# Gathering the last rows of eight experts by quarter, and starting a quarter's attention when its own tiles are added

## The chip, the cores and the metric

The kernel runs on one core of a Trainium2 chip. The core has five engines that run their own instruction streams: TensorE (PE, matmuls, with its weight loads listed as PEld), VectorE (DVE), ScalarE (ACT), GpSimd (POOL) and SyncE (SP, which here only issues DMA transfers). The metric is the device time of one execution in microseconds (us); lower is better.

## The reference

A residual stream `x` of 4 sequences of 1024 rows of 128 numbers passes four layers. Each layer is `x = norm(x + mixer(x))`, then `x = norm(x + ffn(x))`. The change lies at the seam between the last two layers, so only these matter:

```python
# layer 2, FFN: 8 experts, top 2 of each row
x = _layernorm(x + _L2_ffn_ref(x, ...))
# layer 3, attention: a gated unit whose mixing over time is a Toeplitz product
x = _layernorm(x + _L3_attn_ref(x, ...))
# layer 3, FFN: 32 experts, top 4 of each row, and a shared gated unit
logits = flat @ router_w.T + router_bias
scores = softmax(logits)
topk_scores, topk_idx = top_k(scores, 4)
topk_scores = topk_scores / topk_scores.sum(-1)
h = silu(einsum('nd,ehd->neh', flat, gate_w)) * einsum('nd,ehd->neh', flat, up_w)
expert_out = einsum('neh,edh->ned', h, down_w)
out = sum of the 4 chosen expert_out, times topk_scores
out = out + silu(flat @ sgate_w.T) * (flat @ sup_w.T) @ sdown_w.T
x = _layernorm(x + out)
```

The layer-3 attention takes the first axis, the four sequences, as the axis that it mixes over: a row meets only the rows of the same step in the other sequences. So a quarter of the 1024 steps (256 steps of all four sequences) can pass through it by itself, as soon as all four sequences have those steps. The layer-2 attention before it works along each sequence.

## The kernel before

`x` stays in SBUF as 32 tiles of 128 rows. Eight tiles make a quarter: two of each of the four sequences. All weights are loaded by SP when they are needed.

**Experts.** For an FFN with experts, a part of the rows goes through fixed steps. The router writes, for each row and each of its k choices, a position in a list (`pos...`, written on DVE at L1272) and a weight (`wk...`). `spread` scatters the rows of `x` to the list in DRAM, one POOL transfer of 128 rows for each tile and choice. The experts read the list four tiles at a time (`xg`), one group after the other, and write results to a second list (`yg`). `collect` gathers the results back, again one POOL transfer (L1297) for each tile and choice into a buffer `yt`, and adds them to `x` on DVE with their weights (L1388).

**Parts.** Layer 2 splits the rows three ways: `a2` is the first two quarters of all sequences, `m2` the last two quarters of sequences 0 and 1, `n2` the last two quarters of sequences 2 and 3. With two choices, `n2` has eight tiles and 16 gathers. Its tiles 0 and 1 are the third quarter of sequence 2, tiles 2 and 3 the fourth quarter of sequence 2, tiles 4 and 5 the third quarter of sequence 3, and tiles 6 and 7 the fourth quarter of sequence 3. Layer 3 splits by time: part `a` is quarters one and two, `b` the third quarter, `c` the fourth. A part of layer 3 passes, in this order, `l3_attn` (norm, root mean square, projections, mixing over the sequences, projection, second norm, transposes), `l3_route` (logits, softmax, the mask of the top four, positions), `spread` (64 scatters for `a`, 32 each for `b` and `c`), `l3_shared` (the shared unit, with its products `hs`), `l3_experts` (20 groups for `a`, 12 each for `b` and `c`, then a branch at L1355 for rows that overflow), `collect` and the final norm.

**Order.** Each step is a Python generator that emits some instructions and yields an estimated cost in us. `mix(main, side, pace)` emits the main step and, each time main has spent its cost, as much of the side work. `chain` runs generators one after the other; `abreast` runs several and always continues the one whose sum of costs is smallest. `collect` keeps the gathered tiles in a queue and adds a tile when its gathers are thought to have landed or when the pool's buffers are used up. The engines execute in the emitted order, each its own stream, and wait for each other by semaphores.

The seam looks like this. While `mix` emits the shared unit and the experts of part `a`, the side work is the chain of L1918 to L1927: the collection of `n2`, the attention and the routing of `b`, and what follows.

```python
on = self.chain(
    on, self.rows_in(n2), self.l3_attn(b), self.l3_route(b),
    self.abreast(
        self.chain(self.spread("l3", b, K3), self.when(listed("made l3a")), self.last(a, yp)),
        self.chain(self.l3_attn(c), self.l3_route(c)),
    ),
```

`rows_in(part)` opens a pool of its own with eight buffers on the right side of SBUF and calls `collect`. Such pools are closed again when the part is done, so the next one takes the same memory: the buffers for `n2` lie where those for `m2` lay. `yp` is the pool `l3y`, with eight buffers on the left side, opened just before this chain and used for the collections of layer 3.

The names in the profile: `yt<-l2yn` is a gather of `n2`'s results, `x<-yt,wkl2n` its add; `bn<-x` (L191) is the first instruction of a norm; `lg` are the router's logits (L1658 the sum with the bias, L712 the end of the softmax); `posl3b` are the positions of part b; `l3rb<-x` a scatter of part b's rows; `xg<-l3rb` the load of a group of its list; `gu`, `hg`, `hT` and `yp` are an expert group's products in the order of the work (gate and up, gated, transposed, down).

Of the kernel before, what the change touches and what calls it, by code (L numbers as in the profile page):

```python
# [41 lines left out]
E2, F2, R2, K2 = 8, 512, 16, 2  # L42
# [32 lines left out]
class Kernel:  # L75
# [1298 lines left out]
                        in_=self.zero.unsqueeze(1).to_broadcast([P, tl - at, D]),  # L1374
                    )

    def collect(self, lay, part, k, yp, first=0, nt=None):

        nc = self.nc
        pos, wk = self.route[lay + part.name][:2]  # L1380
        assert f"made {lay}{part.name}" in self.listed
        ys = self.lists[lay, part.name][1]
        late = []

        def add():
            t, yt, _ = late.pop(0)
            for i in range(k):
                nc.vector.scalar_tensor_tensor(  # L1388
                    self.x[:, part.order[t], :], yt[:, i, :], wk[:, t, i : i + 1], self.x[:, part.order[t], :],
                    ALU.mult, ALU.add,  # L1390
                )

        for t in range(first, first + (nt or part.nt)):
            yt = self.tile(yp, [P, k, D], "yt")
            for i in range(k):
                self.indirect(
                    out=yt[:, i, :], out_offset=None, in_=ys,
                    in_offset=bass.IndirectOffsetOnAxis(ap=pos[:, t, i : i + 1], axis=0),
                )

            late.append((t, yt, self.moved_by + 4.0))
            if len(late) == yp.bufs:
                while late[0][2] > self.now:
                    yield (1.0,)
                add()
            yield (1.26 * k,)
        while late:
            while late[0][2] > self.now:
                yield (1.0,)
            add()  # L1410
            yield (0.36 * k,)
# [456 lines left out]
    def all(self):  # L1868
        a, rest = self.first, self.rest
        b, c = rest  # L1870
        r = self.both[1]
        a2, m2, n2 = self.by_rows
        with ExitStack() as ctx:
            lgp = self.pool(ctx, "l2lg")
            self.l2_lg = self.tile(lgp, [P, NT, E2], "lg")
            with ExitStack() as early:

                self.l0_setup(early)
                self.l2_wr = self.load(lgp, self.ins["l2_wr"])
                self.run(self.l0_attn((0, 1)))  # L1880
                self.l1_setup()
                self.l2_setup()
                self.zero_lists("l1")
                self.run(self.l0_ffn((0, 1)))
                self.run(self.l1_attn((0, 1)))

                self.run(self.l1_route(a))
                self.run(self.mix(self.l0_attn((2, 3), True), self.spread("l1", a, K1)))
                self.zero_lists("l2", "l3")
                with ExitStack() as c2:  # L1890
                    wall = self.l1_wall(c2)
                    yp = self.pool(c2, "l1ya", 5, right=True)
                    side = self.chain(self.l0_ffn((2, 3), True), self.l1_attn((2, 3), True))
                    self.run(self.mix(self.chain(self.l1_shared(a), self.l1_experts(a, wall)), side, 2.0, False))
                    self.run(self.mix(self.abreast(self.l2_weights(), side), self.l1_close(a, yp)))
            with ExitStack() as c2:
                wall = self.l1_wall(c2)
                self.run(self.mix(self.l2_attn(0), self.chain(self.l1_route(r), self.spread("l1", r, K1))))
                wall2 = self.l2_wall(c2)
                yp = self.pool(c2, "l1yr", 5, right=True)  # L1900
                self.run(self.mix(self.chain(self.l1_experts(r, wall), self.l1_shared(r)), self.routed(a2)))
                self.run(self.mix(self.l2_experts(a2, wall2), self.l1_close(r, yp)))
            listed = lambda name: lambda: name in self.listed
            on = self.served(
                self.chain(self.rows_in(a2), self.onward(a, True)),
                (lambda: self.rows_done >= B + 2, self.routed(m2)),
                (lambda: self.rows_done == 2 * B, self.routed(n2)),
            )
            self.run(self.mix(self.l2_attn(1), on, drain=False))
            with ExitStack() as c3:  # L1910
                with ExitStack() as c2:
                    wall = self.l2_wall(c2)
                    self.press(on, listed("l2m"))
                    self.run(self.mix(self.l2_experts(m2, wall), on, drain=False))
                    self.press(on, lambda: {"l2n", "routed l3a"} <= self.listed)
                    sw, wall3 = self.l3_wall(c3, True)
                    on = self.chain(on, self.rows_in(m2))
                    self.run(self.mix(self.l2_experts(n2, wall), on, drain=False))  # L1918
                self.press(on, listed("l3a"))
                yp = self.pool(c3, "l3y", 8)  # L1920
                on = self.chain(
                    on, self.rows_in(n2), self.l3_attn(b), self.l3_route(b),
                    self.abreast(
                        self.chain(self.spread("l3", b, K3), self.when(listed("made l3a")), self.last(a, yp)),
                        self.chain(self.l3_attn(c), self.l3_route(c)),
                    ),
                    self.spread("l3", c, K3), self.when(listed("made l3b")), self.last(b, yp),  # L1927
                )
                self.run(self.mix(self.chain(self.l3_shared(a, sw), self.l3_experts(a, wall3)), on, 0.75, False))
                self.press(on, listed("l3b"))  # L1930
                self.run(self.mix(self.chain(self.l3_shared(b, sw), self.l3_experts(b, wall3)), on, 0.75, False))
                self.press(on, listed("l3c"))
                self.run(self.mix(self.chain(self.l3_shared(c, sw), self.l3_experts(c, wall3)), on))
                self.run(self.close(c, yp))
        bad = self.nc.values_load(self.flag[0:1, 0:1], min_val=0, max_val=1)
        with self.tc.If(bad > 0):
            with ExitStack() as ctx:
                lgp = self.pool(ctx, "l2lg2")
                self.l2_lg = self.tile(lgp, [P, NT, E2], "lg")
                self.l2_wr = self.load(lgp, self.ins["l2_wr"])  # L1940
                self.l2_attn_general()
                for p in self.by_rows:
                    self.run(self.routed(p))
                    with ExitStack() as c2:
                        self.run(self.l2_experts(p, self.l2_wall(c2)))
                    self.run(self.rows_in(p))
                for p in self.parts:
                    self.run(self.onward(p))
                    with ExitStack() as c2:
                        sw, wall = self.l3_wall(c2)  # L1950
                        self.run(self.l3_shared(p, sw), self.l3_experts(p, wall))
                        self.run(self.last(p, self.pool(c2, "l3y" + p.name, 5)))
# [165 lines left out]
```

## Time and profile before

| | us |
|---|---|
| median of three runs | 2064.29 |
| lowest, highest | 2057.93, 2067.41 |
| profiled execution, its own time | 2440.36 |
| its span, first to last instruction | 2438.2 |
| PE busy in the span | 1619.9 |
| DVE busy | 1303.3 |
| ACT busy | 789.9 |
| POOL busy | 774.0 |

The profile is one execution with the recorder on. It took 376 us, or 18%, more than the median, so its times place the work and size the steps, and only their sum can be held against its own 2440.36 us. A line of a list of groups gives the source line, the engine, the operation, output and inputs with their names, and how many; in a timeline the first two numbers are start and length in us, and a number in brackets is idle time of that engine just before, with what ended it.

The last stages in that execution: shared unit of part a until 1935.3 us; experts of part a 1941.5 to 2034.1; routing of part b until 2063.7; scatters of part b 2064.1 to 2105.1; experts of part b 2109.6 to 2231; gathers of part a 2105.4 to 2228.3; scatters of part c 2228.6 to 2273.1; gathers of part b 2273.4 to 2313.2; experts of part c until 2379.6; gathers of part c 2384.3 to 2424.

### The profile page before, as it was taken

Reading aid. Unit: us, or ns where it says so; the run is one execution under the profiler, and the core shown is the slowest. Engines: PE = TensorE matmul, PEld = TensorE weight load, DVE = VectorE, ACT = ScalarE, POOL = GpSimd, SP = SyncE. Lnnn points to the kernel's source line nnn. Section 1 sums busy time; section 2 is a strip of 40 time slices with the busy share of each in tenths; the row PEclk is TensorE's granted clock in tenths of the full one; section 3 lists DMA queues with packets and bytes.
Section 4 is the critical chain, followed back from the end, with each engine's and each line's share of the span. In section 5 each row is a group of like instructions: output and inputs, shape, how many; then the busy total and the mean of one; then the engine's idle time right before and its main releaser. Section 6 shows DMA issues by size and latency. Waiting matters only on the chain. (4 is left out here: it accounts for less than half of the span.)

```text
span 2438.2 us, 27135 instructions
## 1 busy us (share of the span) xinstructions
PE 1619.9 (66%) x9017; PEld 962.6 (39%) x9017; DVE 1303.3 (53%) x3732; ACT 789.9 (32%) x1114; POOL 774.0 (32%) x701
## 2 busy tenths in 40 slices
PE   7535776875661775687968787887853898267080
PEld 3214333753320344545623232345532586154070
DVE  8767795655570564324535665464711378247053
ACT  5511372322230432222336454642211254122030
POOL 5531285145227002224132002002164201736704
PEclk9766787988785888888979898988876998577595
DMA  9930002334101014312120000031141141223132
GB/s 308 288 104 0 13 33 82 117 120 159 60 31 52 14 73 142 100 48 70 44 96 21 1 1 17 2 117 35 42 174 40 44 127 45 71 71 96 51 100 59
DMA packets 215530, 187.10 MB, mean 77 GB/s; under 512 B 16528, under 2 KB 194064, under 8 KB 214864
## 3 DMA queue, kind: packets, MB, share of 16 engines
q1 hardware_dynamic: 194672, 142.29, 18.5%
q0 software_dynamic: 20704, 42.86, 5.7%
q8 instruction: 84, 1.38, 0.2%
q14 instruction: 70, 0.57, 0.1%
HBM read 88.49 MB, written 96.60 MB: 76 GB/s over the span
## 5 line engine op out<-in xcount | busy, mean ns | idle before, releaser
L1051 ACT ACTIVATE pr<-sc 128x1024 f32<-128x1024 f32 x288 | 279.6, 1021 | 326.1 <-PE sc L157 197.7
L157 PE MATMUL gu<-ld,xgT 128*128 x640 | 172.1, 413 | 81.9 <-issue 36.6
L157 PE MATMUL sc<-qm,kT 32*128 32x512 f32 (+3 forms) x1536 | 200.2, 564 | 15.9 <-ACT pr L1051 12.0
L157 PE MATMUL s<-pr,va 128*32 128x512 f32 (+3 forms) x1536 | 177.3, 531 | 46.0 <-issue 27.9
L157 PEld LDWEIGHTS gu<-ld,xgT 128*128 128x128 f32 x640 | 123.6, 204 | 109.5 <-issue 48.0
L157 PE MATMUL gu<-wall,xgT 128*128 x304 | 161.0, 657 | 3.2 <-ACT xgT L167 2.0
L1057 DVE TENSOR_TENSOR pr<-pr,ld 128x512 f32<-128x512 f32 (+1 forms) x160 | 92.5, 581 | 101.3 <-ACT pr L1051 98.8
L169 DVE COPY hT<-tp 128x512 f32<-128x512 f32 x118 | 81.0, 686 | 120.7 <-PE tp L165 50.4
L165 PE MATMUL tp<-ld,hg 128*128 128x128 f32 x624 | 100.6, 285 | 50.4 <-DVE hT L169 35.4
L157 PEld LDWEIGHTS sc<-qm,kT 32*128 32x128 f32 x1536 | 85.5, 200 | 119.5 <-issue 66.6
L165 PE MATMUL tp<-ld,xg 128*128 128x128 f32 x396 | 66.3, 295 | 90.9 <-issue 50.7
L165 PEld LDWEIGHTS tp<-ld,hg 128*128 128x128 f32 x624 | 80.1, 147 | 104.8 <-DVE hT L169 42.2
L167 ACT COPY xgT<-tp 128x512 f32<-128x512 f32 x99 | 58.0, 587 | 195.4 <-PE tp L165 126.9
L1730 DVE TENSOR_TENSOR hg<-sg,gu 128x256 f32<-128x256 f32 x160 | 65.7, 416 | 102.5 <-ACT sg L1729 94.8
L1494 ACT ACTIVATE sg<-gu 128x512 f32<-128x512 f32 x76 | 45.2, 597 | 226.3 <-PE gu L157 115.3
L1297 POOL DMA_INDIRECT l1ra<-x,posl1a x64 | 95.6, 1494 | 60.5 <-DVE posl1a L1272 41.3
L1729 ACT ACTIVATE sg<-gu 128x256 f32<-128x256 f32 x160 | 60.6, 384 | 157.3 <-PE gu L157 85.7
L157 PE MATMUL pu<-xT,ld 128*128 128x512 f32 x104 | 65.0, 719 | 60.1 <-issue 58.5
L1297 POOL DMA_INDIRECT yt<-l1yr,posl1r x64 | 60.7, 948 | 139.2 <-DVE x L1388 78.8
L157 PEld LDWEIGHTS s<-pr,va 128*32 128x32 f32 x1536 | 38.7, 113 | 156.6 <-issue 110.6
L1496 DVE TENSOR_TENSOR hg<-sg,gu 128x512 f32<-128x512 f32 x76 | 51.8, 681 | 87.2 <-ACT sg L1494 43.9
L1297 POOL DMA_INDIRECT l1rr<-x,posl1r x64 | 61.7, 964 | 99.6 <-DVE posl1r L1272 80.4
(443 smaller groups left out, 3551.7 us busy)
## 6 DMA issues: line engine op xcount, KB each, us to landing
wall<-wall SPq DMA_DIRECT2D x16, 768.0 KB
l3ra<-zero SPq DMA_DIRECT2D x1, 6144.0 KB
ld<-in_l_w SPq DMA_DIRECT2D x2, 3072.0 KB
wall<-we SPq DMA_DIRECT2D x24, 256.0 KB
ld<-in_l_w SPq DMA_DIRECT2D x1, 6144.0 KB
l1ra<-zero SPq DMA_DIRECT2D x1, 5120.0 KB
l1rr<-zero SPq DMA_DIRECT2D x1, 5120.0 KB
xg<-l3ra SPq DMA_DIRECT2D x20, 256.0 KB
```

Of the source, the lines that this page charges most:

```text
L157: return self.nc.tensor.matmul(out, lhsT, rhs, start=start, stop=stop)
L165: nc.tensor.transpose(pt[:, k * P : (k + 1) * P], s, self.ident)
L167: nc.scalar.copy(dst, pt[:, : n * P])
L169: nc.vector.tensor_copy(dst, pt[:, : n * P])
L1051: nc.scalar.activation(pr, sc[h], AF.Exp)
L1057: nc.vector.tensor_tensor(d, d, cst["tril"].unsqueeze(1).unsqueeze(1).to_broadcast([P, 2, n, P]), ALU.mult)
L1297: ins = self.nc.gpsimd.indirect_dma_start(**kw)
L1494: nc.scalar.activation(sg, gu[:, 0, :], AF.Silu)
L1496: nc.vector.tensor_tensor(h, sg, gu[:, 1, :], ALU.mult)
L1729: nc.scalar.activation(sg, pg[:, :, 0, :], AF.Silu)
L1730: nc.vector.tensor_tensor(h[:, 2 * c : 2 * c + 2, :], sg, pg[:, :, 1, :], ALU.mult)
```

## The change

`collect` takes a list of tiles. The chain of L1918 no longer calls `rows_in(n2)`. It collects the four tiles of the third quarter first; then the attention and the routing of part b run abreast with the collection of the four tiles of the fourth quarter. Both collections use the pool `yp` instead of a pool of their own.

```diff
-    def collect(self, lay, part, k, yp, first=0, nt=None):
+    def collect(self, lay, part, k, yp, first=0, nt=None, which=None):
...
-        for t in range(first, first + (nt or part.nt)):
+        for t in which or range(first, first + (nt or part.nt)):
             yt = self.tile(yp, [P, k, D], "yt")
...
                 yp = self.pool(c3, "l3y", 8)
+
                 on = self.chain(
-                    on, self.rows_in(n2), self.l3_attn(b), self.l3_route(b),
+                    on, self.collect("l2", n2, K2, yp, which=(0, 1, 4, 5)),
+                    self.abreast(
+                        self.chain(self.l3_attn(b), self.l3_route(b)),
+                        self.collect("l2", n2, K2, yp, which=(2, 3, 6, 7)),
+                    ),
                     self.abreast(
                         self.chain(self.spread("l3", b, K3), self.when(listed("made l3a")), self.last(a, yp)),
                         self.chain(self.l3_attn(c), self.l3_route(c)),
```

## The prediction

> **What bounds the kernel now.** I read the page's totals first, then the windows of the last 650 us, then one tile's waits, then timelines around the two edges of the change.
>
> ```profile
> PE 1619.9 (66%) x9017; PEld 962.6 (39%) x9017; DVE 1303.3 (53%) x3732; ACT 789.9 (32%) x1114; POOL 774.0 (32%) x701
> q8 instruction: 84, 1.38, 0.2%
> ```
>
> No engine is busy throughout, so the bound must be read stage by stage. The rows below give a stretch, its length, and the busy us of PE, weight loads, DVE, ACT and POOL.
>
> ```profile
> 1800.00:1864.00 64.00, 6.97 (x31) 4.54 (x29) 2.66 (x4) 1.99 (x4) 48.11 (x51) 0.59 0.15 52
> 1893.00:1916.00 23.00, 23.00 (x102) 14.15 (x103) 7.31 (x12) 5.38 (x9) 0.00 (x0) 1.00 0.04 12
> 1916.00:1938.00 22.00, 19.13 (x92) 12.29 (x90) 8.64 (x20) 4.18 (x7) 11.47 (x12) 1.00 0.14 37
> 1941.00:2034.00 93.00, 87.16 (x536) 75.06 (x536) 64.12 (x169) 46.71 (x88) 3.06 (x4) 0.96 0.37 112
> 2036.00:2064.00 28.00, 24.64 (x89) 15.53 (x90) 22.08 (x110) 12.56 (x18) 0.00 (x0) 0.76 0.03 7
> 2064.00:2106.00 42.00, 15.51 (x58) 8.37 (x56) 12.57 (x27) 7.75 (x12) 32.15 (x33) 0.71 0.16 60
> ```
>
> Part a's 20 expert groups (1941 to 2034) are PE's: 87 us busy of 93. Then from 2036 to 2064 the path is part b's attention tail and routing on DVE, and from 2064 to 2106 POOL's scatters of part b's rows. What releases POOL there decides:
>
> ```profile
> L1297 POOL DMA_INDIRECT l3rb<-x,posl3b x32: 957/962/1262, 2064.1 to 2104.2; - x32
>   DVE posl3b L1272: 119.1, 1
> ```
>
> POOL stood idle 119.1 us for the positions of part b. After the scatters the expert inputs are loaded at 2106.5 and the rest (experts b, gathers a, scatters c, experts c, gathers c) follows in a chain. So the time moves with posl3b, at 2063.67. The timelines (start, length) show what sets it:
>
> ```profile
> 1969.95 0.34 DVE L1388 SCALAR_TENSOR_TENSOR x<-yt,wkl2n,x 128x128 f32<-128x128 f32 x1
> 1970.21 0.29 DVE L191 BATCH_NORM_STATS2 bn<-x 128x6 f32<-128x128 f32 x1
> ...
> 2046.56 0.42 DVE L1658 TENSOR_TENSOR lg<-s,rows 128x256 f32<-128x256 f32 x1 [0.88 <-PE s L157]
> 2049.77 0.42 DVE L712 TENSOR_TENSOR lg<-lg,red 128x256 f32<-128x256 f32 x1
> 2063.67 0.16 DVE L1272 TENSOR_SCALAR posl3b<-pm 128x32 uint32<-128x32 f32 x1
> ```
> ```profile
> 2033.05 1.06 PE L157 MATMUL yp<-ld,hT 128*128 x8
> 2039.36 2.18 PE L165 MATMUL s<-ld,x 128*128 128x128 f32 x8 [5.25 <-DVE x L205]
> ```
>
> The attention's first norm starts at 1970.2, behind the last of n2's 32 adds. Paced beside the experts, it is not done when PE finishes them (2034.1): its second norm still runs, PE waits 5.25 us for it, and transposes, logits and softmax follow with little cover.
>
> **What the Trainium skill says.** "Perfetto Trace Analysis", DMA Instruction — SWDGE (GPSIMD): the recorded end of such a POOL transfer is the end of descriptor generation, not the data's arrival. The trace agrees: the first gather of the last collection is recorded from 2384.25 for 0.95 us, and its add starts at 2386.83. So buffers free up later than POOL's rows tell. "ScalarE: Activation LUTs", What ACT_TABLE_LOAD costs: about 1.28 us a load plus a 1.38 us drain. The loads here are 1.28 us (1973.49, 1975.10); no separate drain shows (1973.49 + 1.28 = 1974.77, next activation at 1974.78), so I use 1.28. "Runtime: NRT & Kernel Launch", Instruction fetch mechanics: instructions stream in 16 KiB blocks over a DMA queue of the sequencer's own, mostly hidden. Block size agrees (1.38 MB / 84 = 16.4 KB). "Mostly hidden" does not hold beside POOL bursts: PE idles 54.0 us under "issue" at 2258.9, until part b's gathers end. That the burst delays the fetch is my inference.
>
> **The change, part by part.** The instruction list is the same on every engine within five; what changes is order, buffers and waits.
>
> Gathers: the 16 gathers of n2 (2 per tile, 1.25 us apart) stay in place on POOL, third-quarter tiles first. Their eight buffers now come from the left-side pool of the later gathers, not from the memory in which m2's rows lay. Before, they waited for DVE's adds of m2's rows:
>
> ```profile
> 1916.63 0.95 POOL L1297 DMA_INDIRECT yt<-l2yn,posl2n  x1 [53.29 <-DVE x L1388]
> 1927.07 1.07 POOL L1297 DMA_INDIRECT yt<-l2yn,posl2n  x1 [5.75 <-DVE x L1388]
> ```
>
> Afterwards the first needs only the list's last write (issued 1892.6, so about 1895), and all 16 can go in one run of 16 × 1.25 = 20 us, 1895 to 1915. Nothing on POOL is behind them until part b's scatters. Direct worth: zero, since DVE takes the rows up from 1955.8. Bounds: a gain of about 3, as the hold of the first expert input (last shared matmul about 1935.3, load issued 1938.53) ends just after today's burst; a loss is rival 2.
>
> Attention start: before, 16 adds of the fourth and third quarters lie in five batches behind groups' hT copies from 1955.8 to 1970.4. Afterwards the eight third-quarter adds go behind the first groups' copies and the norm starts behind the fourth group's, which in today's clock is about 1958.6: 11.6 us, 3.3 groups of 3.54 us. Its weights' loads (l3_uv, l3_o; 1970.59 and 1971.07) move on SP ahead of later expert-input loads, and there wait only for m2's gathers, done at 1863: cost zero, two issues of 0.38 us on a queue with a 3.5 us period. If that queue were late, the fourth input load slips by under 1 us.
>
> The other eight adds: 8 × 0.27 = 2.2 us, now between the attention's rms steps, where DVE is nearly full (1970 to 1992: 17.9 busy of 21.8). The lead at the attention's end is 11.6 − 2.2 = about 9.5 us, before the branch that ends the experts (L1355).
>
> PE: eight transposes (about 0.9 us beside the expert stream) and eight logits matmuls (0.8) come ahead of the last `yp`: experts end at 2034.1 + 1.7. Table loads: the second norm's sqrt pair moves inside group 18; two loads, 2 × 1.28, half covered by the rotation of two buffers: +1.3. So about 2037.1. Then, in a row: lg add .42, reduce .41, subtract .42 behind it, load for exp 1.28, exp .42, reduce .41, reciprocal .20 = 3.6: L712 at 2040.7 against 2049.77, 9.1 earlier.
>
> L712 to posl3b took 13.9 us; five `hs` products of 0.69 lay in it and about 1.7 us of waits for PE. Those waits shrink, one product falls out, or neither: 11.6 to 13.9. posl3b at 2052.3 to 2054.6, an advance of 9.1 to 11.4; I take 10. If DVE's 5 us of second norm stays ahead of the branch's wait, 5; if the hold at 1935 goes too, about 14.
>
> Downstream it carries one to one: 32 scatters at 1.266 = 40.5 us need nothing else (POOL had been idle), part b's shared matmuls (26 us of PE) lie under them, then inputs, gathers (64 × 1.25 = 80), scatters c, experts c. What is late next is POOL.
>
> **Sum.** 2440.4 (span 2438.2) − 10 = 2430.4. The profiled execution is 376 us, 18%, above the median of 2064.3; which stages swell isn't shown. The stretch concerned has almost no POOL work and few idle gaps, so I carry the 10 us over whole; scaled by 2064/2440 it would be 8.5. Taken: 2054.
>
> **Rivals.**
> 1. The lead is eaten in the expert stage. For: DVE has 64 us busy of 93, 82% where the attention is dense, and each group waits for ACT's and DVE's turns. If the moved table loads, eight x-norms (2.1 us) and 2.2 us of adds stretch the groups in full, 10 − 1.3 − 2.1 − 2.2 = about 4 are left: 2060. Against: PE's idle in the stage is only 6 us, so most of DVE's work does fit.
> 2. Slower: the unbroken gather run of 1895 to 1915 falls on part a's shared matmuls, where PE is now 23.0 busy of 23, and starves PE or DVE of instructions. From 1824 to 1865 PE was busy 1.04 us of 41 beside 32 gathers. If PE stops for the run, up to 20 us are lost and the 10 gained don't pay: 2074. Decides when PE's busy share there falls below half. Against: beside today's 12 gathers (1916 to 1938) PE kept 19.1 of 22.
> 3. More: the hold at 1935 goes (3), PE's clock (0.76 after the branch) stays up because PE has no 5.25 us gap, and part c, ahead by the same order, also leaves its holds: 14 to 20 us, 2047.
> 4. It does nothing: posl3b doesn't move since routing is bound by the shared matmuls' `hs` on DVE; 2064. Against: they take 5 × 0.69 of 13.9.
>
> **How the numbers follow.** Forecast case 0.45 (2049 to 2059), rival 1 0.17, rival 2 0.16, rival 3 0.16, rival 4 0.06. A measurement of this kernel tells about 0.5%, 10.3 us, from no change. The forecast lies on that edge: three fifths of its chance counts as faster, two fifths as same. Faster: 0.27 + 0.16 and 0.02 of rival 1 = 0.45. Same: 0.18 + 0.15 + 0.06 less 0.02 of rival 4's tail = 0.37. Slower: 0.16 + 0.02 = 0.18. The range, 2041 to 2072, leaves out the upper part of rival 2 and the end of rival 3.
>
> **What would show it.** Right: gathers of l2yn in one run from about 1895; first BATCH_NORM_STATS2 after them near 1958; L1658 ahead of the branch; PE's 5.25 us wait gone; posl3b some 10 us before 2063.7, and every later stage by as much. Wrong: PE's idle between 1893 and 1938 above 3 us (rival 2), groups in 1941 to 2034 longer than 93 us in all by over 5 (rival 1), or posl3b early and the end not, which would put the bound on something I did not see behind it.

## The result, and the profile after

The changed kernel takes 2051.16 us (median of ten runs, 2045.74 to 2057.39), the kernel before 2060.54 (2051.75 to 2067.41). The ratio is 0.9958, interval 0.9940 to 0.9977: about 8.7 us faster, somewhere between 4.7 and 12.4.

The profile that the prediction was read from shows an execution of 2440 us, in a condition that these timed runs do not share, so below the changed kernel (its profiled execution took 2053.12 us, span 2051.1) is compared with a second profile of the kernel before, of 2055.36 us (span 2053.2). Both lie within the range of the timed runs, so the recorder is not what costs 18%.

The two spans differ by only 2.1 us, less than the 8.7 of the timed runs: part a's positions were written at 1530.6 us in the one and at 1535.0 in the other, ahead of everything that the change touches. Times are therefore counted from the load of part a's first expert input (1646.2 before, 1650.8 after). From there to the end of the span it is 407.0 us before and 400.3 after, 6.7 us less, which lies within the interval of the timed gain.

First the page's totals, before (second profile) and then after, and for the latter one of its two instruction queues (packets, MB, share).

```profile
PE 1542.9 (75%) x9017; PEld 930.7 (45%) x9017; DVE 1302.4 (63%) x3732; ACT 789.6 (38%) x1114; POOL 778.8 (38%) x701
```
```profile
PE 1542.7 (75%) x9017; PEld 927.7 (45%) x9017; DVE 1303.3 (64%) x3732; ACT 787.6 (38%) x1113; POOL 777.9 (38%) x701
q8 instruction: 84, 1.38, 0.3%
```

The engines do the same work; it only lies elsewhere. Next the stretches of the last gathers and shared unit, the experts of part a, the routing of part b, its scatters: before, then after (stretch, length, busy us of PE, weight loads, DVE, ACT, POOL, each with its count, then PE's granted clock as a share of full speed, the busy share of the DMA engines and GB/s).

```profile
1617.00:1646.20 29.20, 19.36 (x86) 12.33 (x86) 9.27 (x22) 3.58 (x6) 22.19 (x24) 0.76 0.20 55
1646.20:1742.70 96.50, 86.99 (x536) 74.70 (x536) 66.93 (x179) 47.65 (x90) 9.68 (x11) 0.96 0.40 118
1742.70:1771.00 28.30, 24.03 (x88) 15.27 (x89) 22.67 (x116) 13.23 (x18) 0.00 (x0) 0.76 0.05 13
1771.00:1813.00 42.00, 15.28 (x58) 8.47 (x56) 12.77 (x28) 7.96 (x12) 31.91 (x33) 0.70 0.16 59
```
```profile
1621.60:1650.80 29.20, 19.82 (x86) 12.52 (x86) 9.24 (x21) 3.58 (x6) 22.02 (x24) 0.75 0.18 53
1650.80:1751.70 100.90, 90.32 (x560) 77.36 (x560) 74.99 (x222) 52.72 (x97) 9.43 (x10) 0.97 0.38 114
1751.70:1768.00 16.30, 14.14 (x48) 8.00 (x49) 13.88 (x71) 5.52 (x8) 0.00 (x0) 0.79 0.06 18
1768.00:1810.00 42.00, 20.25 (x75) 11.22 (x74) 13.91 (x29) 8.69 (x13) 32.11 (x33) 0.76 0.17 60
```

Some 4 us more pass in the expert stage and 12 fewer in the routing. PE's records beside the experts rise from 536 to 560: eight transposes, and eight logits matmuls with two records each. DVE takes on 8.1 us in the stage (66.93 to 74.99), which grows by 4.4.

The edges of the change on DVE and PE, before (two views) and after (two views):

```profile
1677.81 0.29 DVE L191 BATCH_NORM_STATS2 bn<-x 128x6 f32<-128x128 f32 x1
...
1754.16 0.42 DVE L1658 TENSOR_TENSOR lg<-s,rows 128x256 f32<-128x256 f32 x1 [0.88 <-PE s L157]
1757.37 0.42 DVE L712 TENSOR_TENSOR lg<-lg,red 128x256 f32<-128x256 f32 x1
1770.89 0.16 DVE L1272 TENSOR_SCALAR posl3b<-pm 128x32 uint32<-128x32 f32 x1
```
```profile
1746.97 2.18 PE L165 MATMUL s<-ld,x 128*128 128x128 f32 x8 [5.27 <-DVE x L205]
```
```profile
1670.65 0.28 DVE L191 BATCH_NORM_STATS2 bn<-x 128x6 f32<-128x128 f32 x1
...
1749.68 0.42 DVE L1658 TENSOR_TENSOR lg<-s,rows 128x256 f32<-128x256 f32 x1 [1.01 <-PE s L157]
1753.80 0.43 DVE L712 TENSOR_TENSOR lg<-lg,red 128x256 f32<-128x256 f32 x1
1767.68 0.18 DVE L1272 TENSOR_SCALAR posl3b<-pm 128x32 uint32<-128x32 f32 x1
```
```profile
1745.57 1.04 PE L165 MATMUL s<-ld,x 128*128 128x128 f32 x8
1746.44 0.60 PE L165 MATMUL tp<-ld,hg 128*128 128x128 f32 x4
1746.88 1.06 PE L157 MATMUL yp<-ld,hT 128*128 x8
1747.77 1.87 PE L157 MATMUL s<-ld,xT 128*128 128x32 f32 x16
1749.47 1.14 PE L157 MATMUL yp<-ld,hT 128*128 x8
1753.86 2.05 PE L157 MATMUL pg<-xT,ld 128*128 128x512 f32 x2 [3.25 <-DVEq L1355]
```

Subtract the first input's load and the rows line up: the norm starts at 31.6 before and 19.9 after, L1658 at 108.0 and 98.9, L712 at 111.2 and 103.0, posl3b at 124.7 and 116.9. PE's 5.27 us wait for the attention is gone; in its place it waits 3.25 us at the branch for DVE (DVEq is DVE's instruction sequencer, L1355 the branch).

The first gather of n2, before and then after:

```profile
1639.27 0.95 POOL L1297 DMA_INDIRECT yt<-l2yn,posl2n  x1 [0.30 <-DVE x L1388]
```
```profile
1643.41 0.97 POOL L1297 DMA_INDIRECT yt<-l2yn,posl2n  x1 [0.30 <-PE pu L157]
```

It follows the last gather of m2 after 0.30 us in both, and the other fifteen follow it about 1.25 us apart. In neither kernel does POOL wait for DVE's adds of m2's rows here: the 53.29 us that the prediction showed belongs to the other condition. The scatters of part b answer for what follows.

```profile
L1297 POOL DMA_INDIRECT l3rb<-x,posl3b x32: 954/958/1260, 1771.3 to 1811.3; - x32
  DVE posl3b L1272: 112.4, 1
```
```profile
L1297 POOL DMA_INDIRECT l3rb<-x,posl3b x32: 954/958/1436, 1768.1 to 1807.9; - x32
  DVE posl3b L1272: 105.0, 1
```

They start at 125.2 before and 117.3 after, from the first expert input. From posl3b to the end of the span it is 282.3 us before and 283.4 after.

### The profile page after: what moved, and what is told of

The parts are those of the page before. It is cut to its first block, busy times and chain, and to the rows that moved or that the text cites. A ratio compares the mean times of both kernels' runs of the same rounds, so it can differ in the third digit from the quotient of the medians.

```text
span 2051.1 us, 27115 instructions
## 1 busy us (share of the span) xinstructions
PE 1542.7 (75%) x9017; PEld 927.7 (45%) x9017; DVE 1303.3 (64%) x3732; ACT 787.6 (38%) x1113; POOL 777.9 (38%) x701
## 2 busy tenths in 40 slices
DMA packets 215530, 187.10 MB, mean 91 GB/s; under 512 B 16528, under 2 KB 194064, under 8 KB 214864
## 5 line engine op out<-in xcount | busy, mean ns | idle before, releaser
L157 PE MATMUL sc<-qm,kT 32*128 32x512 f32 (+3 forms) x1536 | 190.0, 551 | 1.0 <-ACT pr L1051 1.0
L157 PE MATMUL gu<-ld,xgT 128*128 x640 | 167.2, 404 | 24.1 <-DVE hg L1730 12.5
L157 PE MATMUL s<-pr,va 128*32 128x512 f32 (+3 forms) x1536 | 164.7, 524 | 17.7 <-DVE x L989 7.3
L157 PE MATMUL gu<-wall,xgT 128*128 x304 | 147.8, 610 | 3.2 <-ACT xgT L167 2.0
L165 PE MATMUL tp<-ld,hg 128*128 128x128 f32 x624 | 96.3, 276 | 2.8 <-DVE hT L169 2.7
L1297 POOL DMA_INDIRECT l2rm<-x,posl2m x16 | 15.7, 984 | 200.4 <-DVE posl2m L1272 195.8
L1297 POOL DMA_INDIRECT l3ra<-x,posl3a x64 | 61.5, 962 | 77.1 <-DVE posl3a L1272 51.0
L157 PE MATMUL yp<-ld,hT 128*128 x640 | 86.0, 277 | 2.4 <-DVE hT L169 1.5
## 6 DMA issues: line engine op xcount, KB each, us to landing
wall<-wall SPq DMA_DIRECT2D x16, 768.0 KB, 10.6
ld<-in_l_w SPq DMA_DIRECT2D x2, 3072.0 KB, 13.5
```

The lines of the kernel that those rows point to most:

```text
L157: return self.nc.tensor.matmul(out, lhsT, rhs, start=start, stop=stop)
L165: nc.tensor.transpose(pt[:, k * P : (k + 1) * P], s, self.ident)
L1297: ins = self.nc.gpsimd.indirect_dma_start(**kw)
```

## The experiments

All ratios are to the kernel before in the same comparison. "posl3b at" is counted from the load of part a's first expert input.

**The kernel before once more.** No edit.

> The kernel before once more, for a profile that stands nearer to the timed runs than the one shown. Theory (the attention's lead sets posl3b): posl3b is written 8 to 11 us later, counted from the first expert input of part a, than in the changed kernel (113.4 us), so at 121 to 125; from posl3b to the end of the span as in the changed kernel, 283 us within 3. Rival (the freed gathers bring the gain): posl3b at 113 to 116 after the first expert input, and the shared unit of part a ends its first-input hold some 5 to 9 us later.

posl3b at 124.7, changed kernel 116.9: 7.8 us later, just under the 8 to 11 expected. The 113.4 us in the expectation was counted from PE's first transposes, 3.5 us after the load; the comparison is unaffected. From posl3b to the end it is 282.3, as expected. The theory holds; that the freed gathers bring the gain does not.

**Buffers and order apart.** Three kernels take the change's two halves apart.

```diff
 # only the buffers
-    on, self.rows_in(n2), self.l3_attn(b), self.l3_route(b),
+    on, self.collect("l2", n2, K2, yp), self.l3_attn(b), self.l3_route(b),
```

> Only the buffers change: n2's rows are collected in the old order and wholly ahead of the attention, but into the pool of layer 3, so the 16 gathers need not wait for DVE's adds of m2's rows. Theory (the attention's lead is the gain): ratio to before 0.999 to 1.001, at most 3 us faster by the hold ahead of the first expert input. Rival A (the freed gathers are the gain): 0.995 to 0.997. Rival B (the unbroken run of gathers starves the shared unit): 1.003 or more.

Ratio 1.0003 (0.9991 to 1.0016), posl3b at 125.1. The buffers are worth nothing here, where the kernel before does not wait for them.

```diff
 # only the order: a right-side pool as in rows_in
+    def split_in(self, part, b):
+        with ExitStack() as ctx:
+            yp = self.pool(ctx, "l2y" + part.name, 8, right=True)
+            yield from self.collect("l2", part, K2, yp, which=(0, 1, 4, 5))
+            yield from self.abreast(
+                self.chain(self.l3_attn(b), self.l3_route(b)),
+                self.collect("l2", part, K2, yp, which=(2, 3, 6, 7)),
+            )
...
-    on, self.collect("l2", n2, K2, yp, which=(0, 1, 4, 5)),
-    self.abreast(
-        self.chain(self.l3_attn(b), self.l3_route(b)),
-        self.collect("l2", n2, K2, yp, which=(2, 3, 6, 7)),
-    ),
+    on, self.split_in(n2, b),
```

> Only the order changes: third quarter first, attention begun when its own tiles are added, but the gathers keep a right-side pool of their own where m2's buffers lay and wait for DVE's adds as before. Theory (lead): ratio 0.995 to 0.997, the whole gain or all but 1 to 3 us of it. Rival A (freed gathers): 0.999 to 1.001, since the late gathers hold the adds and so the attention.

Ratio 0.9952 (0.9935 to 0.9970), posl3b at 116.1. The order brings the whole gain.

> The changed kernel once more, on the chip of the two partial kernels. Both theories: ratio 0.994 to 0.998, as measured first (0.9958). If the lead and the buffers add up, its gain is the sum of the gains of the two partial kernels within 2 us.

Ratio 0.9957 (0.9937 to 0.9978), posl3b at 117.0. In us of 2060.43: the buffers lose 0.6, the order gains 9.9, both together gain 8.9. They add up within the expected 2 us, though each of these figures is uncertain by 3 to 4 us; posl3b (125.1, 116.1, 117.0) tells the same more sharply.

```diff
 # third quarter first, but the attention behind all eight tiles
-    on, self.collect("l2", n2, K2, yp, which=(0, 1, 4, 5)),
-    self.abreast(
-        self.chain(self.l3_attn(b), self.l3_route(b)),
-        self.collect("l2", n2, K2, yp, which=(2, 3, 6, 7)),
-    ),
+    on, self.collect("l2", n2, K2, yp, which=(0, 1, 4, 5, 2, 3, 6, 7)),
+    self.l3_attn(b), self.l3_route(b),
```

> The changed kernel with the tiles in the new order and the pool of layer 3, but the attention of part b held back until all eight tiles of n2 are added. Theory (what counts is that the attention starts behind four tiles): the gain is gone, ratio to before 0.999 to 1.002, posl3b 124 to 126 us after the load of part a's first expert input (before 124.7, changed kernel 116.9). Rival (having the third quarter first is enough): ratio near 0.996, posl3b at 117 to 119.

Ratio 1.0013 (0.9997 to 1.0029), posl3b at 124.8. Gathering the third quarter first does nothing by itself; beginning the attention behind its four tiles brings the gain.

**The price of the eight later adds.** They are held back by a condition on the emission.

```diff
-            while late[0][2] > self.now:
+            while late[0][2] > self.now or not (until is None or until()):
...
-    self.collect("l2", n2, K2, yp, which=(2, 3, 6, 7)),
+    self.collect("l2", n2, K2, yp, which=(2, 3, 6, 7), until=lambda: self.now >= 1454.0),
```

> The changed kernel with the eight adds of the fourth quarter moved from the attention's root-mean-square steps to its mixing steps some seven groups later. If the adds cost the attention their own 2.2 us, as the prediction has it: posl3b 114.5 to 115.5 us after the first expert input and a ratio near 0.9947. If DVE's gaps hide them: 116.5 to 117.5 and 0.9957, as in the changed kernel.

posl3b at 117.0, ratio 0.9954 (0.9938 to 0.9970). Moved by some seven groups they change nothing at the end. Nor do they at the place that they leave: from the start of the norm to the end of the rms steps it takes 19.0 us in the changed kernel, 18.8 with the adds moved away, and 19.0 in the kernel before, where all but one are done when the norm begins.

**More lead.** Two ways to begin or finish the attention still earlier. `land` is the time that `collect` allows a gather before its add.

```diff
-    on, self.collect("l2", n2, K2, yp, which=(0, 1, 4, 5)),
+    on, self.collect("l2", n2, K2, yp, which=(0, 1, 4, 5), land=-5.0),   # was 4.0
```

> The changed kernel with the first four tiles' adds placed earlier (their assumed landing 9 us sooner), so that the attention starts two groups earlier. Theory (the lead carries over one to one): 2 x 3.5 = 7 us more, posl3b 109 to 112 us after the first expert input, ratio 0.992 to 0.993. Rival A (the expert stage has no room for more, the lead is eaten): posl3b 115 to 118, ratio 0.995 to 0.997. Rival B (the adds now wait for their gathers and hold the groups' DVE work): expert stage of part a longer by 3 us or more, ratio 0.997 or more.

```diff
-    self.run(self.mix(self.chain(self.l3_shared(a, sw), self.l3_experts(a, wall3)), on, 0.75, False))
+    self.run(self.mix(self.chain(self.l3_shared(a, sw), self.l3_experts(a, wall3)), on, 0.6, False))
```

> The changed kernel with the pace of the work beside part a's shared unit and experts changed from 0.75 to 0.6, so that more of the attention is placed beside each group. Theory (lead): the routing is placed 63 x 0.2 = 12.6 us of main work earlier, of which the denser groups give back 3 to 6: posl3b 106 to 112, ratio 0.990 to 0.994. Rival (DVE has no room): the last store of part a's experts goes from 100.5 to 106 or later, posl3b 114 or later, ratio 0.995 or more.

The earlier start: the norm begins at 13.6 instead of 19.9, 6.3 us sooner, and posl3b comes at 115.3, only 1.6 sooner. Ratio 0.9954 (0.9934 to 0.9974). The last store of the experts moves from 100.5 to 104.3. The other pace: posl3b at 114.4, last store at 106.6, ratio 0.9953 (0.9933 to 0.9974). The expert stages, the earlier start first:

```profile
1662.10:1766.40 104.30, 91.95 (x560) 78.92 (x560) 78.78 (x247) 54.59 (x99) 9.44 (x10) 0.95 0.37 110
```
```profile
1646.70:1753.40 106.70, 93.86 (x565) 79.35 (x564) 81.87 (x263) 55.44 (x100) 9.55 (x11) 0.95 0.36 107
```

DVE's busy time in the stage (the third of the busy times) goes from 74.99 in the changed kernel to 78.78 and 81.87, PE's idle time from 10.6 to 12.4 and 12.8. The stage stretches with what is put into it. Rival A of the earlier start holds. The stage's growth of 3.9 us is also the sign that was named for rival B, but no add waits for its gathers in that trace, and the ratio is not B's. For the other pace all three signs of its rival came, but not quite for its reason:

```profile
1760.58 0.69 DVE L736 TENSOR_TENSOR hs<-sg,pu 128x512 f32<-128x512 f32 x1 [2.58 <-issue]
```

L712 came at 93.2, 9.8 us sooner than in the changed kernel, so the lead is still there at that point. The tail behind L712 then took 21.3 us instead of 13.9. Most of it lies beside the last groups, and at its end DVE stands idle for 2.58 us ahead of this one product of the shared unit, which needs a matmul that ends at 1760.48 and comes just ahead of posl3b (1761.19). The other pace was not run with the products moved behind posl3b. Also, the scatters of b ran slower at their end (one took 3.26 us at 1800.6), so that expert inputs b were loaded no sooner (159.8) than in the changed kernel (159.5). Neither edit gains beyond the changed kernel anything that the timed runs can tell, and both write part c's positions 12 to 13 us later (243.0 and 242.2 against 230.0).

**The routing tail.** The shared unit's products of part b are tied behind posl3b on DVE.

```diff
-        nc.vector.tensor_tensor(dst, sg, pu, ALU.mult)
+        hs = nc.vector.tensor_tensor(dst, sg, pu, ALU.mult)
+        if behind is not None:      # self.placed, the write of posl3b, for part b
+            self.tc.add_manual_dep(hs.ins, behind.ins.name, ..., reason="queued behind")
```

> The changed kernel with the shared unit's products (hs) of part b held behind posl3b on DVE, so that none of them lies in the routing tail; part a's expert stage is as in the changed kernel. Theory (the tail's products and their waits are on the path, and what posl3b gains the end gains): 4 x 0.69 = 2.8 us of products and up to 1.9 us of waits for PE leave the tail, posl3b 112 to 114 us after the first expert input (changed kernel 116.9), from posl3b to the end still 281 to 285 us, ratio 0.993 to 0.995. Rival (the shared unit, begun later, becomes late for the scatters or the expert inputs): posl3b as early, but the end not: posl3b to the end 286 us or more, ratio 0.996 or more.

posl3b at 115.6, only 1.3 sooner, not 3 to 5; from posl3b to the end 283.7; ratio 0.9940 (0.9924 to 0.9956). The value is the lowest ratio of all, but its interval overlaps that of the changed kernel. With the products gone the tail still takes 12.1 us from L712, against 13.9: what is left waits for itself (short dependent DVE steps) and for PE, as this line of its DVE timeline shows.

```profile
1756.44 0.42 DVE L1248 COPY ptot<-s 128x256 f32<-128x256 f32 x1 [1.91 <-PE s L157]
```

**The table loads of the second norm.**

```diff
-    self.norm(self.quarter(q), by="dve" if exps else "act")
+    self.norm(self.quarter(q), by="dve" if exps or part.name == "b" else "act")
```

> The changed kernel with the reciprocal root of part b's second norm computed on DVE (some 15 small operations of about 0.15 us) in place of ACT's square root, so that its two table loads leave the last groups of part a's experts. If the loads are what stretches the stage beyond the moved matmuls: last store of part a's experts 98 to 99 us after the first expert input (changed kernel 100.5, before 96.1). If it is the DVE work and the matmuls: 100 to 102. Ratio in either case within 0.002 of the changed kernel's.

Last store at 101.5, ratio 0.9955 (0.9934 to 0.9975). Without the loads the stage is not shorter, so they are not shown to be what stretches it; the added DVE work may hide a saving of theirs. The run shows another thing: the second norm ends 3.8 us later than in the changed kernel (96.1 against 92.3), and posl3b is still written at 117.0. So either most of these 3.8 us of lead are of no use in the changed kernel, or the loads that are gone make up for them; L1658 comes 1.1 us later.

**What is late next.** Two kernels move 16 of part a's gathers behind part c's scatters, alone and with the products behind and the earlier start.

```diff
-    self.chain(self.spread("l3", b, K3), self.when(listed("made l3a")), self.last(a, yp)),
+    self.chain(self.spread("l3", b, K3), self.when(listed("made l3a")), self.collect("l3", a, K3, yp, 0, 12)),
     self.chain(self.l3_attn(c), self.l3_route(c)),
...
-    self.spread("l3", c, K3), self.when(listed("made l3b")), self.last(b, yp),
+    self.spread("l3", c, K3), self.collect("l3", a, K3, yp, 12, 4), self.finish(a),
+    self.when(listed("made l3b")), self.last(b, yp),
```

> The changed kernel with the last 16 of part a's 64 gathers placed behind part c's 32 scatters on POOL. It asks what is late once posl3b is early. Theory (POOL's queue, not the routing of c, sets the start of part c's experts): in the changed kernel posl3c is ready 230 us after the first expert input and the scatters start at 246, so they can start up to 16 us earlier; the 16 gathers (20 us) then lie under part c's experts; end 10 to 16 us earlier than the changed kernel, ratio 0.988 to 0.991. Rival (experts of part b on PE, or the moved gathers, become late instead): less than 5 us, ratio 0.9935 or more.

> The reordered gathers of part a, the shared unit's products behind posl3b, and the attention two groups earlier, together on the changed kernel. If the steps add up: posl3b 113 to 114.5 us after the first expert input (changed kernel 116.9, with the products behind 115.6, with the earlier start 115.3), and 2 to 4 us beyond what the reordered gathers alone give; if the scatters of c then wait for posl3c instead, no more than these alone give.

In this comparison the kernel before itself took 2439.77 us, so neither the 16 us nor the sum of the steps was put to the test that was meant. The ratios are 1.0055 (1.0037 to 1.0073) and 1.0083 (1.0053 to 1.0113), slower than the kernel before; the changed kernel itself was not timed in this condition, so how much of that is due to the change and how much to the later edits stays open, as does what the reordered gathers gain at 2060 us. Two things can be read. In both traces the scatters of c now start within 0.5 us of posl3c (282.5 behind 282.1, and 285.3 behind 284.9), so POOL's queue no longer holds them. And posl3b comes at 116.3 and, with all steps together, at 114.2, within the 113 to 114.5 expected of them.

The traces say something else, too. The streams of the first are those of the changed kernel until well past posl3b, so up to there it shows the changed kernel in the condition of the profile that the prediction was read from. In the views, "issue" stands for a wait for nothing that the profile shows, "remote" for a release that the profile puts down to no instruction of this core. On POOL and DVE:

```profile
1889.60 0.94 POOL L1297 DMA_INDIRECT yt<-l2yn,posl2n  x1 [29.71 <-DMA l2yn<-yg]
...
1908.32 0.94 POOL L1297 DMA_INDIRECT yt<-l2yn,posl2n  x1 [0.30 <-issue]
```
```profile
1894.07 0.69 DVE L736 TENSOR_TENSOR hs<-sg,pu 128x512 f32<-128x512 f32 x1 [1.03 <-PE pu L157]
1912.38 0.69 DVE L1687 TENSOR_TENSOR x<-py,x 128x512 f32<-128x512 f32 x1 [17.62 <-remote]
```

All 16 gathers run unbroken from 1889.6 to 1909.3, and DVE stands for 17.62 us under "remote", until 1912.4; PE meanwhile stands for 11.90 us, waiting for a product of DVE's. From part a's positions to the first expert input it takes 193.3 us against 184.6 in the first profile of the kernel before: 8.7 us lost. From there to posl3b it takes 116.3 against 125.1: 8.9 us gained. The trace of the steps together repeats it (DVE stands 16.81 us, 195.7 us to the first expert input). By these traces, two after the change against one before it, the prediction's slower rival takes back in that condition what its forecast brings.

## Why the prediction was right or wrong

Forecast was a gain of 10 us, with posl3b and all behind it sooner by as much; measured were 8.7 us in the timed runs and 7.8 at posl3b. The mechanism is the one forecast: the four kernels with and without the buffers and the order, and the one whose attention waits for all eight tiles, leave none of the other causes named. The terms:

| step | forecast, us | measured, us |
|---|---|---|
| attention's norm starts earlier by | 11.6 | 11.8 |
| second norm ends earlier by | 9.5 | 10.1 (102.4 to 92.3) |
| experts of part a longer by | 3.0 | 4.3 at the last store (96.2 to 100.5) |
| L1658 earlier by | 9.5 (2046.6 to 2037.1) | 9.1 |
| L712 earlier by | 9.1 | 8.2 |
| L712 to posl3b shorter by | 0 to 2.3 | longer by 0.4 (13.5 to 13.9) |
| posl3b earlier by | 9.1 to 11.4, 10 taken | 7.8 |
| posl3b to the end | unchanged | 282.3 to 283.4 |

Three terms were mis-sized. The eight logits matmuls were put at 0.8 us; the row after shows them as 16 records of 1.87 us together, and the profile that the prediction read has them as two rows of eight (1.78 and 1.75 us). That would account for 1.1 of the 1.3 us that the stage grew beyond the forecast, but it costs posl3b little, since L1658 comes nearly as early as forecast. Of the 0.9 us missing at L712, 0.5 lies in the softmax between the two, put at 3.6 us and measured at 4.1. The tail from L712 to posl3b was credited with up to 2.3 us for products that fall out or wait less. One of the five did fall out, and still the tail kept its length: the shared unit cannot start before the branch, where PE waits 3.25 us for DVE, and its products arrive late again. Even without any of them the tail loses only 1.8 us. Against this stands a cost that isn't there: the eight adds at 2.2 us were charged to the attention, but from the start of the norm to the end of the rms steps it takes 19.0 us with and without them, so they fit into DVE's gaps.

Some of the prediction's readings were slips that did not carry the result. n2 has 16 adds, not 32, as the prediction itself counts further down. The 32 POOL transfers from 1824 to 1865 are 16 gathers and as many scatters of part a. And of the two instruction queues on the page only q8 has blocks of 16.4 KB; q14 moved 0.57 MB in 70 packets, 8.1 KB each.

**The buffers** were given no direct worth, with a gain of 3 us as the bound. Zero is right for the timed runs, but not for the reason given. The wait of 53.29 us and the hold of 3.2 us at 1935 do not exist in the second profile of the kernel before: the gathers follow m2's without a pause there, and the first expert input is loaded as soon as the shared unit ends.

**Rival 1**, the lead eaten, holds for most of any lead beyond this change. Of 6.3 us more at the start of the norm, 3.3 are left at L1658 and 1.6 reach posl3b. Of the 9.8 us that the other pace gains at L712, 2.4 reach posl3b: there it is the tail that eats the lead, more than the expert stage that the rival named. The change took the lead that the tail could still use, and not much is left behind it.

**Rival 2**, the unbroken gathers starving the shared unit, did not occur in the timed runs: PE is busy 19.8 us of 29.2 in that stretch after the change and 19.4 before, and the buffers alone give 1.0003. It did occur, at 8.7 of its up to 20 us, in the one condition in which "issue" and "remote" waits appear beside POOL's work, which was the condition of the profile that it was argued from. The Trainium skill ("Runtime: NRT & Kernel Launch", Instruction fetch mechanics) calls the cost of fetching the next block mostly hidden; in the second profile of the kernel before, PE's longest wait under "issue" is 7.3 us, in the first 54.0. Fetching itself was not measured, so the cause of these waits stays an inference.

**The step from 2440 us to 2064** carried the 10 us over whole, since the stretch has little POOL work. The lead agrees: 7.8 us in the timed runs' condition and 8.9 in the long one. But the sum for the end was made in a profile in whose condition the same change comes to about nothing at posl3b (8.7 lost, 8.9 gained). That the sum fits the timed runs is in part luck: by these traces it would not have held in the condition that it was worked out for, and the charge for the adds and the credit for the tail were wrong in opposite ways. A gap of 18% between the profiled execution and the median should have been taken as a sign that some of its waits are not in the timed runs, and the waits named "issue" and "remote" were the ones to take out first.

**Rivals 3 and 4** fall. PE's clock after the branch went only from 0.76 to 0.79, the hold at 1935 was not there to be gained, and the scatters of part c start only 4.7 us earlier (250.6 to 245.9). And posl3b did move.

## What to carry to other kernels

Where a stage is pinned by one engine and the next by a chain that waits for a side task, start the side task as soon as its own inputs are there; the order of the transfers alone brings nothing, nor do buffers that were not waited for. The gain ends where the pinned stage grows by what is moved into it, or where the chain behind waits for something else, so count both (here 3.3 us of PE and 8.1 of DVE lengthened the stage by 4.4, and of 6.3 us of further lead 1.6 arrived). Hold a profile against the timed runs before costing waits from it: if it is 18% longer, its long waits may belong to its condition alone.

## What the runs showed of the hardware that was not expected

One program took 2060 us in one comparison and 2440 in another, with the same instructions, the same busy time of DVE (1302.4 and 1303.3 us) and the same bytes moved (187.10 MB). The chip does not tell them apart: the comparison with the products behind posl3b (2060.93 us for the kernel before) and the last one (2439.77) both ran on chip number 10. PE is busy 77 us longer (1619.9 against 1542.9) at a mean granted clock of 0.81 in place of 0.87. The rest shows for the most part as idle time beside POOL's transfers, named "issue" on PE (up to 54.0 us at once) and "remote" on DVE and ACT (17.62 and 16.34 us beside 16 gathers): in the three traces of that condition every such wait of over 10 us on these engines lies beside them, and at 2060 us no trace has a "remote" wait of over 1.5 us on DVE or ACT. In the last kernel, whose shared unit of part b lies later in POOL's transfers because its products are behind posl3b, the next expert input was loaded 57 us after the last scatter's start (211.6 against 154.2). With the reordered gathers alone, in the same condition, it was 2.4 us (158.4 against 156.0), and with the products behind alone, in the other condition, 2.4 us as well (157.8 against 155.4). What sets the condition isn't known from these runs.
